# Load queue, PSUM eviction by pairs and a third result buffer in a 7x7 depthwise stage

## The chip, the cores and the metric

The kernel runs on one core of a Trainium2 chip. The metric is the device time of one execution in microseconds. TensorE (PE) multiplies, VectorE (DVE) and ScalarE (ACT) read its results out of PSUM, GpSimd (POOL) moves data inside SBUF, and SyncE (SP) issues DMAs. SP, ACT and POOL each have a DMA queue of their own; all three queues are served by the same 16 DMA engines.

## The reference

Two layers on one image of 384 channels of 192x192 in float32. The first is a group norm, a 1x1 convolution, a 2x2 max pool, a 3x3 depthwise convolution and a channel attention. The second, which the change touches, is a group norm and a 7x7 depthwise convolution with symmetrised weights:

```python
    x = x + _L0_conv_ref(_gn(x), ...)
    # --- layer 1 (conv_preact) ---
    x = x + _L1_conv_ref(_gn(x), L1_conv_weight)

    def _L1_conv_ref(x, weight):
        w_sym = (weight + jnp.rot90(weight, k=1, axes=(2, 3)) + jnp.rot90(weight, k=2, axes=(2, 3)) + jnp.rot90(weight, k=3, axes=(2, 3))) * 0.25
        return _dwconv(x, w_sym, STRIDE, PAD)
```

## The kernel before, in words

The first layer takes about 2490 us and ends by writing the sum x to DRAM twice: `sd` holds it in the order that the 7x7 stage wants (128 rows of "column phase and image row", each with 384 channels of 300 numbers), and `sh` holds the halo rows. The 7x7 weights lie in DRAM as `wt`, one banded matrix of 128x384 per channel.

The 7x7 stage runs 48 steps of eight channels. For each channel, three float32 matmuls (L825, L830, L836; each of them is two passes of the PE array) add up one result of 128x288 in PSUM: two multiply the weights with shifted views of the main operand, the third multiplies with `aux`, which holds halo rows and a constant row. Two channels share one PSUM tile `pc` of two banks, and there are four such tiles, one for each pair q of a step.

Step n does this, in the order in which the code records it (`keep` holds each engine to this order):

- The loads for step n+2 are issued: `w` (L677, 1536 KB, 128 pieces of 12,288 bytes), `main` (L682, 1200 KB, 128 pieces of 9,600 bytes) and two halo loads into `aux` (L687, 281 KB each, 30 pieces of 9,600 bytes). There are three buffers of each.
- POOL prepares step n+1 (`borders`, L749 to L770): it adds the mean at the borders of `main` and `aux` and copies a part of `main` into `aux`.
- POOL turns the results of step n-1 into rows (`spread`, two copies from `apart` to `res`, L794), and eight stores write them out (L798, 144 KB each in pieces of 768 bytes; `res` has two buffers).
- PE computes the four pairs. Each pair is read out of PSUM in four parts of 32 partitions (g = 0 to 3) that are scaled and stored in `apart`; DVE takes g = 0 and 2 (L849), ACT takes g = 1 and 3 (L847). `apart` has two buffers.
- After the second pair, DVE adds the identity to the weights of step n+1 (`middle`, L784).

All loads and stores of this stage are on SP's queue, so SP issues w, main, two halos, eight stores, w, main and so on. A DMA reports its end on one of eight semaphores that are handed round in turn; a DMA that gets a semaphore still in use waits, before it is issued, for the DMA eight places earlier to land. In the program before, a step has twelve DMAs, and the fifth to eighth store of a step wait in this way for the landing of that step's w, main and halos.

Of the kernel before, what the change touches and what calls it, by code (L numbers as in the profile page):

```python
# [8 lines left out]
F32 = mybir.dt.float32  # L9
# [4 lines left out]
P = 128  # L14
# [38 lines left out]
NT = HW // TR  # L53
CP = 4
NJ = HW // CP
# [19 lines left out]
def conv_preact_d2(  # L75
# [17 lines left out]
    nc = tc.nc  # L93
# [10 lines left out]
    sd = dram.tile([CP * TR, C, RUN], F32, name="sd")  # L104
# [3 lines left out]
    wt = dram.tile([P, C, 3 * P], F32, name="wt")  # L108
# [13 lines left out]
    for kt in range(KT):  # L122
        g = gsel[:, kt, :].rearrange("p (g j) -> p g j", j=GC)
# [136 lines left out]
    with ExitStack() as bx:  # L260
# [70 lines left out]
        for r in range(3):  # L331
            row = []
            for ct in range(CT):
                t = padp.tile([P, PR + 2, PS + 2], F32, name=f"pad{r}_{ct}")
# [208 lines left out]
    with ExitStack() as dx:  # L543
# [8 lines left out]
        for i in range(4):  # L552
            t = sxp.tile([P, LEAD + CP * RB * RUN + LEAD], F32, name=f"sx{i}")
# [97 lines left out]
    with ExitStack() as ex_:  # L651
# [3 lines left out]
        outp = ex_.enter_context(tc.tile_pool(name="outp", bufs=2))  # L655
        auxs = []
        for i in range(3):
            t = wide.tile([P, CB, NT, JP], F32, name=f"aux{i}")
# [10 lines left out]
        keep = tc.keep_in_program_order  # L669
        steps = C // CB  # L670

        def span(n):
            return slice(n * CB, (n + 1) * CB)

        def load_w(n):
            w = wtp.tile([P, CB, 3 * P], F32, name=f"w{n}", tag="w")
            keep(nc.sync.dma_start(w, wt[:, span(n)]))  # L677
            return w

        def load_main(n):  # L680
            main = mainp.tile([P, CB, NT, JP], F32, name=f"main{n}", tag="main")
            keep(nc.sync.dma_start(main.rearrange("p c t j -> p c (t j)"), sd[:, span(n)]))  # L682
            aux = auxs[n % len(auxs)]
            af = aux.rearrange("p c t j -> p c (t j)")
            for base, h in ((TOP, 0), (BOT, HALO)):
                keep(
                    nc.sync.dma_start(  # L687
                        af[base : base + HALO * NQ], sh[h * NQ : (h + HALO) * NQ, span(n)]
                    )
                )  # L690
            return main, aux

        ws = {n: load_w(n) for n in range(2)}
        mains = {n: load_main(n) for n in range(2)}

        mean1, rstd1, _ = group_stats(st.rearrange("p t b n s -> p t (b n) s"), "1")
# [17 lines left out]
        with tc.tile_pool(name="mps", bufs=1, space=PSUM) as mps:  # L714
            rows = []
            for name, v in (("mb", mean1), ("sb", std1), ("rb", rstd1)):
                t = wide.tile([P, C], F32, name=name)
# [23 lines left out]
        def borders(n):  # L741

            main, aux = mains[n]
            cs = span(n)

            def border(t, lo, hi, j, k, nj):
                part = t[lo:hi, :, :, j : j + nj]
                keep(
                    nc.gpsimd.tensor_tensor(  # L749
                        part, part,  # L750
                        mm[lo:hi, cs, k : k + nj].unsqueeze(2).to_broadcast(
                            [hi - lo, CB, NT, nj]
                        ),
                        ALU.add,
                    )
                )

            border(main, 0, P, 0, 0, 1)
            border(main, 0, P, NJ, 1, 2)
            keep(  # L760
                nc.gpsimd.tensor_copy(
                    aux[0:TOP, :, :, 0:NJ].rearrange("p c t j -> p (c t) j"),
                    main[0:TOP, :, :, 2 : 2 + NJ].rearrange("p c t j -> p (c t) j"),
                )
            )
            border(aux, TOP, ONE, 0, 3, 1)
            border(aux, TOP, ONE, NJ - 1, 4, 1)
            for base, t in ((TOP, 0), (BOT, NT - 1)):
                keep(
                    nc.gpsimd.tensor_copy(  # L770
                        aux[base : base + HALO * NQ, :, t, 0:NJ],
                        mb[base : base + HALO * NQ, cs].unsqueeze(2).to_broadcast(
                            [HALO * NQ, CB, NJ]
                        ),
                    )
                )

        def middle(n):

            for i in range(0, CB, 4):  # L780
                c = n * CB + i
                mid = ws[n][:, i : i + 4, CENTRE : CENTRE + P]
                keep(
                    nc.vector.scalar_tensor_tensor(  # L784
                        mid, eye.unsqueeze(1).to_broadcast([P, 4, P]), stdb[:, c : c + 1], mid,
                        ALU.mult, ALU.add,
                    )
                )

        def spread(n, apart):  # L790

            res = outp.tile([P, 2, NT * NJ, CP], F32, name=f"res{n}", tag="res")
            for k in range(2):
                keep(nc.gpsimd.tensor_copy(res[:, k], apart[:, :, k].rearrange("p e n -> p n e")))  # L794
            for k in range(2):
                for q in range(CP):
                    keep(
                        nc.sync.dma_start(  # L798
                            out[n * CB + 2 * q + k].rearrange("(t r) w -> r t w", t=NT),
                            res[q * TR : (q + 1) * TR, k].rearrange(  # L800
                                "p (t j) e -> p t (j e)", t=NT
                            ),
                        )
                    )
# [4 lines left out]
        for n in range(steps):  # L809
            if n + 2 < steps:  # L810
                ws[n + 2] = load_w(n + 2)
                mains[n + 2] = load_main(n + 2)
            if n + 1 < steps:
                borders(n + 1)
            if last is not None:
                spread(n - 1, last)
            w, (main, aux) = ws.pop(n), mains.pop(n)
            apart = outp.tile([P, CP, 2, NT * NJ], F32, name=f"apart{n}", tag="apart")
            for q in range(CP):
                ps = pc.tile([P, 2, 512], F32, name=f"pc{n}_{q}", tag="pc")  # L820
                for k in range(2):
                    i = 2 * q + k
                    acc = ps[:, k, 0 : NT * NJ]
                    keep(
                        nc.tensor.matmul(  # L825
                            acc, w[:, i, 0:P], main[:, i, :, 0:NJ], start=True, stop=False
                        )
                    )
                    keep(
                        nc.tensor.matmul(  # L830
                            acc, w[:, i, P : 2 * P], main[:, i, :, 1 : 1 + NJ],
                            start=False, stop=False,
                        )
                    )
                    keep(
                        nc.tensor.matmul(  # L836
                            acc, w[0:KLAST, i, 2 * P :], aux[0:KLAST, i, :, 0:NJ],
                            start=False, stop=True,
                        )
                    )  # L840
                c = n * CB + 2 * q
                for g in range(CP):
                    src = ps[g * TR : (g + 1) * TR, :, 0 : NT * NJ]
                    dst = apart[q * TR : (q + 1) * TR, CP - 1 - g]
                    scale = rb[g * TR : (g + 1) * TR, c : c + 1]
                    if g % 2:
                        keep(nc.scalar.mul(dst, src, scale))  # L847
                    else:
                        keep(nc.vector.tensor_scalar_mul(dst, src, scale))  # L849
                if q == 1 and n + 1 < steps:  # L850
                    middle(n + 1)
            last = apart
# [57 lines left out]
```

## Time and profile before

| what | value |
|---|---|
| median of 3 runs | 3200.5 us (3199.22 to 3203.96) |
| the profiled execution | 3205.75 us, of which its span is 3204.1 us |
| 7x7 stage, first matmul to end of span | 2534.1 to 3204.1 us |
| PE over the span | 84% busy |
| DVE, ACT, POOL over the span | 77%, 23%, 25% busy |
| DMA on SP's queue | 395.82 MB, 35.7% of the 16 engines' span |

Busy time is time in which an engine executes; waits and DMA issues are not in it. The DMA share is the mean busy share of the 16 DMA engines. The profiled execution is 5.25 us above the median of the runs, so a difference worked out in its trace is applied to the median.

### The profile page before, as it was taken

What the parts mean: (1) busy time and instruction counts of PE and PEld (TensorE: products, weight loads), DVE (VectorE), ACT (ScalarE), POOL (GpSimd) and SP (SyncE); (2) the same over time, 40 slices, a digit from 0 to 9 for tenths busy, and PEclk for the clock granted to TensorE, in tenths of its full rate; (3) what the DMA queues carried; (4) which work ended last, traced back from release to release, by engine and by line L of the source; (5) the groups of instructions that cost most, each with busy time, mean ns of one, the idle gap of its engine ahead of it and who ended that gap; (6) DMA issues with size and microseconds to landing.
All of it is one profiled execution on the core that took longest, in us unless ns stands there. A gap on an engine that the chain in (4) does not pass through costs nothing. (4 is left out here: it accounts for less than half of the span.)

```text
span 3204.1 us, 25358 instructions
## 1 busy us (share of the span) xinstructions
PE 2698.8 (84%) x8243; PEld 1529.8 (48%) x8243; DVE 2466.5 (77%) x3993; ACT 740.1 (23%) x1545; POOL 804.1 (25%) x959
## 2 busy tenths in 40 slices
PE   0079999999999999999999998355784599898997
PEld 0044444444444444444444444234562476666665
DVE  7957878888888877778888888775999676656665
ACT  0001222222222222222222222011211144434443
POOL 0044343100000000000000001143122366667666
PEclk9999999999999999999999999577997699999998
DMA  9946666311111111111111000399999699999998
GB/s 376 372 138 229 208 215 223 103 40 61 46 37 37 37 37 37 37 38 39 38 37 53 27 8 14 124 392 391 362 364 314 213 325 333 320 317 332 328 322 272
DMA packets 205379, 576.50 MB, mean 180 GB/s; under 512 B 18672, under 2 KB 131680, under 8 KB 190080
## 3 DMA queue, kind: packets, MB, share of 16 engines
q1 hardware_dynamic: 156496, 395.82, 35.7%
q0 software_dynamic: 43776, 175.52, 15.8%
q10 hardware_dynamic: 4976, 3.56, 0.3%
q8 instruction: 66, 1.08, 0.1%
q14 instruction: 65, 0.53, 0.1%
HBM read 341.56 MB, written 233.10 MB: 179 GB/s over the span
## 5 line engine op out<-in xcount | busy, mean ns | idle before, releaser
L348 PE MATMUL pq<-xq,wq 128*128 128x512 f32 x3402 | 1474.0, 592 | 0.0
L348 PEld LDWEIGHTS pq<-xq,wq 128*128 128x128 f32 x3402 | 640.0, 190 | 773.5 <-issue 719.2
L384 DVE SCALAR_TENSOR_TENSOR qk<-pad,wd,qk 128x384 f32<-128x384 f32 x1152 | 690.6, 617 | 52.9 <-ACT pad L363 40.7
L355 DVE TENSOR_REDUCE t<-pq 128x128 f32<-128x512 f32 x648 | 444.9, 687 | 253.4 <-PE pq L348 253.4
L849 DVE TENSOR_SCALAR apart<-pc,rb 32x576 f32<-32x576 f32 x384 | 311.1, 810 | 245.3 <-ACT apart L847 156.7
L438 POOL DMA_DIRECT2D vd<-vb x72 | 57.7, 802 | 1350.4 <-DVE vb L384 1350.4
L847 ACT ACTIVATE apart<-pc,rb 32x576 f32<-32x576 f32 x384 | 281.7, 734 | 446.1 <-DVE apart L849 362.3
L384 DVE SCALAR_TENSOR_TENSOR vb<-pad,wd,vb 128x384 f32<-128x384 f32 x576 | 337.5, 614 | 20.5 <-ACT pad L363 18.5
L836 PE MATMUL pc<-aux,w 127*128 127x288 f32 x768 | 262.1, 423 | 42.4 <-POOL aux L770 42.3
L363 ACT ACTIVATE pad<-t,bq 128x96 f32<-128x96 f32 x207 | 77.9, 376 | 931.6 <-DVE t L355 931.6
L608 DVE TENSOR_TENSOR sx<-xr,y 128x576 f32<-128x576 f32 x192 | 222.3, 1212 | 74.9 <-ACT y L597 39.1
L825 PE MATMUL pc<-main,w 128*128 128x288 f32 x768 | 260.3, 421 | 19.5 <-DVE w L784 9.6
L830 PE MATMUL pc<-main,w 128*128 128x288 f32 x768 | 258.6, 419 | 0.0
L348 PE MATMUL pq<-xs,wq 128*128 128x512 f32 x486 | 215.3, 603 | 0.0
L794 POOL COPY res<-apart 128x1152 f32<-128x1152 f32 x96 | 210.0, 2220 | 18.6 <-ACT apart L847 8.2
L577 PE MATMUL po<-v,attnT 128*128 128x288 f32 x448 | 126.6, 438 | 89.3 <-DMA v<-vd 84.0
L836 PEld LDWEIGHTS pc<-aux,w 127*128 127x128 f32 x768 | 150.1, 198 | 96.2 <-POOL aux L770 54.1
L190 PE MATMUL gs<-mv,gsel 128*128 128x1 f32 x36 | 8.5, 353 | 220.9 <-DVE mv L180 218.0
L825 PEld LDWEIGHTS pc<-main,w 128*128 128x128 f32 x768 | 149.2, 196 | 70.4 <-POOL res L794 11.7
L590 PE MATMUL pr<-gl,wp 128*128 128x288 f32 x576 | 154.4, 424 | 32.1 <-ACT y L597 32.0
L830 PEld LDWEIGHTS pc<-main,w 128*128 128x128 f32 x768 | 149.9, 195 | 45.1
L615 DVE BATCH_NORM_STATS2 st<-sx 128x6 f32<-128x288 f32 x384 | 149.8, 474 | 0.2
(128 smaller groups left out, 2044.9 us busy)
## 6 DMA issues: line engine op xcount, KB each, us to landing
w<-wt SPq DMA_DIRECT2D x48, 1536.0 KB, 6.8
sd<-sx POOLq DMA_DIRECT2D x96, 600.0 KB, 10.2
main<-sd SPq DMA_DIRECT2D x48, 1200.0 KB, 11.7
xs<-in_x_dram SPq DMA_DIRECT2D x24, 2304.0 KB, 11.6
xr<-in_x_dram SPq DMA_DIRECT2D x48, 1152.0 KB, 27.1
out_dram<-res SPq DMA_DIRECT2D x384, 144.0 KB, 7.2
xq<-in_x_dram SPq DMA_DIRECT2D x21, 2304.0 KB, 8.2
wt<-g POOLq DMA_DIRECT2D x24, 1152.0 KB, 6.7
```

The source lines that it names most:

```text
L348: nc.tensor.matmul(ps, wq[:, kt, ct * P : (ct + 1) * P], rows[:, kt, :, g * 64 : (g + 1) * 64], start=(kt == 0), stop=(kt == KT - 1),)
L355: nc.vector.tensor_reduce(t[:, :, g * 32 : (g + 1) * 32], ps.rearrange("p (h a w b) -> p h w a b", h=PR, a=2, b=2), AX.XY, ALU.max,)
L384: nc.vector.scalar_tensor_tensor(dst, win, w, dst, ALU.mult, ALU.add)
L590: nc.tensor.matmul(ps[:, h, 0:H], wp[:, ct, ot * P : (ot + 1) * P], gl[:, ct, h * H : (h + 1) * H], start=(ct == 0), stop=(ct == KT - 1),)
L608: nc.vector.tensor_tensor(sx[:, v, :, :, dj : dj + NJ], xq[:, :, :, :, e], y[:, :, :, e // 2].unsqueeze(1).to_broadcast([P, RB, NT, NJ]), ...
L615: nc.vector.bn_stats(st[:, ot, b, v * RB + a, :], sx[:, v, a, :, dj : dj + NJ])
L794: keep(nc.gpsimd.tensor_copy(res[:, k], apart[:, :, k].rearrange("p e n -> p n e")))
L825: nc.tensor.matmul(acc, w[:, i, 0:P], main[:, i, :, 0:NJ], start=True, stop=False)
L830: nc.tensor.matmul(acc, w[:, i, P : 2 * P], main[:, i, :, 1 : 1 + NJ], start=False, stop=False,)
L836: nc.tensor.matmul(acc, w[0:KLAST, i, 2 * P :], aux[0:KLAST, i, :, 0:NJ], start=False, stop=True,)
L847: keep(nc.scalar.mul(dst, src, scale))
L849: keep(nc.vector.tensor_scalar_mul(dst, src, scale))
```

## The change

Three edits in the 7x7 stage. The loads of `w` and `main` are issued by ACT instead of SP; halo loads and stores stay with SP. `apart` gets a third buffer. The four parts of a pair are all read out by one engine: DVE for pairs 0 and 2, ACT for pairs 1 and 3.

```diff
         def load_w(n):
             w = wtp.tile([P, CB, 3 * P], F32, name=f"w{n}", tag="w")
-            keep(nc.sync.dma_start(w, wt[:, span(n)]))
+            keep(nc.scalar.dma_start(w, wt[:, span(n)]))
             return w
 
         def load_main(n):
             main = mainp.tile([P, CB, NT, JP], F32, name=f"main{n}", tag="main")
-            keep(nc.sync.dma_start(main.rearrange("p c t j -> p c (t j)"), sd[:, span(n)]))
+            keep(nc.scalar.dma_start(main.rearrange("p c t j -> p c (t j)"), sd[:, span(n)]))
...
-            apart = outp.tile([P, CP, 2, NT * NJ], F32, name=f"apart{n}", tag="apart")
+            apart = outp.tile([P, CP, 2, NT * NJ], F32, name=f"apart{n}", tag="apart", bufs=3)
...
-                    if g % 2:
+                    if q % 2:
                         keep(nc.scalar.mul(dst, src, scale))
                     else:
                         keep(nc.vector.tensor_scalar_mul(dst, src, scale))
```

In the built program the instructions of PE and POOL stand in the same order as before. ACT's order in a step becomes: issue w(n+2), issue main(n+2), four parts of pair 1, four parts of pair 3. SP's becomes: two halos (n+2), eight stores (n-1). The eight semaphores are handed round in the order halo, w, halo, store 1, main, stores 2 to 8, so that w(n+2) is issued only after the second store of the group before has landed, main(n+2) after its fifth, and the fifth store of a group after that group's first halo, the sixth after its w.

## The prediction

> **What bounds the kernel now.** I read the strip of 40 slices first: from slice 32 on the DMA row stands at 9 and PE at 8 to 9. So I asked for the 7x7 stage alone: busy time by stretch, its DMA queues and issues, and the waits of SP, PE, DVE and ACT.
>
> ```profile
> core 0: us, PE busy (x) PEld busy (x) DVE busy (x) ACT busy (x) POOL busy (x), PEclk, DMA share, GB/s
> 2600.00:2800.00 200.00, 182.02 (x713) 136.28 (x711) 134.23 (x150) 87.82 (x120) 130.17 (x129) 0.97 1.00 326
> 2800.00:3000.00 200.00, 179.07 (x678) 133.76 (x679) 118.06 (x142) 82.48 (x113) 133.65 (x132) 0.94 1.00 325
> 3000.00:3160.00 160.00, 144.82 (x553) 108.54 (x553) 95.09 (x115) 67.57 (x93) 104.72 (x101) 0.95 1.01 329
> ...
> q1 hardware_dynamic: 81745, 182.52, 100.0%
> ...
> w<-wt SPq DMA_DIRECT2D x40, 1536.0 KB, 6.8
> main<-sd SPq DMA_DIRECT2D x40, 1200.0 KB, 11.7
> out_dram<-res SPq DMA_DIRECT2D x320, 144.0 KB, 7.4
> aux<-sh SPq DMA_DIRECT2D x80, 281.2 KB, 12.0
> ```
>
> The reader is to see: all 16 DMA engines are busy all the time (1.00), with SP's queue alone, at 325 to 329 GB/s. A step moves 4.57 MB, so it lasts 14.0 us (w to w in SP's timeline: 2617.30 to 3163.14 in 39 steps). The other engines have room: PE's shortest step is 11.8 us (the last one, 3179.2 to 3191.0), DVE, ACT and POOL are busy 62%, 42% and 66% of these 560 us.
>
> The waits show what DVE and ACT lose to each other, and what holds PE and SP:
>
> ```profile
> ACT apart L847 <- DVE apart L849: 314.7, 247, 4.8
> ...
> DVE apart L849 <- ACT apart L847: 132.2, 162, 0.9
> DVE apart L849 <- POOL res L794: 71.1, 32, 4.6
> ...
> PE pc L836 <- POOL aux L770: 41.9, 23, 3.1
> ```
>
> ```profile
> SPq L798 <- DMA main<-sd: 151.5, 42, 5.8
> SPq L798 <- POOL res L794: 142.6, 50, 5.5
> SPq L798 <- DMA aux<-sh: 49.4, 76, 1.7
> ```
>
> No row has PE waiting for an eviction (L847 or L849). PE waits for POOL's work on halos that landed late. SP's stores wait for loads to land.
>
> How well are the DMA engines used? I counted the trace's DMA packets from 2600 to 3160 us. Pieces of 12,288 bytes (w) take 460 ns at the median and 545 ns in the mean, pieces of 9,600 bytes (main and halos) 366 and 485 ns (361 at the fastest), and 768 bytes (stores) 36 and 40 ns. By the shortest times a step would be (128 x 0.460 + 188 x 0.361 + 1536 x 0.036)/16 = 11.4 us, and 0.1 us for semaphore writes. The 2.5 us above that are 0.7 in w, 1.5 in the 9,600-byte pieces (main's run at 361 to 370 ns, the halos at 600 to 970 ns where they run) and 0.3 in stores. Fewer than 16 packets are in flight in 13% of the time; taken over the engines that is 2.0% of them idle, 0.28 us per step.
>
> **The change part by part.**
>
> *Loads on ACT.* SP loses a w and a main issue per step (0.39 and 0.44 us, its rows at 2784.75 and 2785.18) and ACT gains them: with 8 evictions of 0.734 us, ACT has 6.7 us of work in a step of 14.0. Bytes and pieces stay. Two queues now hold work at once. The trace has such a place, the stretch before, where SP loads xr and POOL stores sd:
>
> ```profile
> 2260.00:2300.00 40.00, 36.92 (x151) 28.05 (x150) 40.00 (x67) 8.05 (x12) 8.98 (x12) 1.00 1.04 354
> ...
> q1 hardware_dynamic: 4376, 7.25, 54.5%
> q0 software_dynamic: 1610, 6.87, 49.5%
> ```
>
> While both queues are full there, packets go one for one whatever their size (in the us from 2289: 59 of 4,800 bytes, 58 of 1,536). So beside w and main, which have 16 pieces per engine, only about 16 of a step's 96 store pieces per engine get through; the rest goes after. That delays stores but leaves no engine idle.
>
> What waits on ACT: w(n+2) for the second store of the previous group, main(n+2) for its fifth. Behind them stand ACT's evictions of step n, and for those wait PE (the pc tiles of pairs 1 and 3) and POOL's res copies. A store alone takes 2.1 us from issue to landing (3196.55 to 3198.63). When the second store lands, up to six more of 0.44 us each (12 pieces of 36 ns) are queued or about to be, 2.6 us of work; a load needs 1.0 us from that landing to its first packet (0.1 wake-up, 0.4 issue, some 0.5 to the first packet, as after the issue at 3196.55). So the DMA engines have cover, and PE has 14.0 - 11.8 = 2.2 us of slack per step. I therefore cost these waits at nothing; without that cover they cost the 1.0 us per step.
>
> The gain is in idle engines. Before, the next w came only after the eighth store was issued, which waited for the second halo (2798.97 landed, 2799.46 w issued), and the engines that were done early had nothing. Now w needs the second store only, and main follows it with no gap. Bounds: 0 to the whole 0.7 us by which w's pieces exceed 460 ns. I take 0.28 us, the idle time counted above, as the row nearest to it: 45 steps x 0.28 = -12.6 us. That two queues slow the pieces is bounded by the two-queue stretch: from 2210 to 2330 us its 4,800-byte pieces took 210 ns (192 at the median), its 1,536-byte ones 74 (65), 9% and 14% above the median, against 10% and 18% for stores and w in one queue now. So I take 0; the bound is 7% of the 7.4 us in which loads and stores mix, +0.5 us per step. The halos still follow the stores on SP's queue and still run mostly among themselves: 0, bounds -0.7 (half of their excess hidden) and +0.5.
>
> A rule speaks against any gain. The Trainium skill, "DMA: Bandwidth & Descriptors", section "Issuing engines are not separate DMA queues", says that DMAs issued from several engines end on the same 16 DMA engines and interleave, so that only the sequencer's issue time is saved. The share of 1.00 with one queue fits it, the 1.04 with two does not quite. By the rule alone the gain would be nothing and the sum +3 us.
>
> *Start of the stage.* w(3) was issued by SP at 2548.47, as the first step's matmuls ended. On ACT it stands behind the four parts of pair 3, 4 x 0.77 = +3.1 us, once; the DMA queue is nearly empty there, so I count +3. Bounds 0 and +3.1.
>
> *Eviction by pairs.* The hand-overs vanish (314.7 us of ACT's idle time, 132.2 of DVE's). Gain on the path: 0, because PE waits for no eviction and the DMA engines set the step. A pair now takes 4 x 0.81 = 3.2 us on DVE or 3.1 on ACT, each engine has two pairs in a step, and with `middle` DVE has 8 us of 14. Without DMA as cover it would be worth at most 2.2 us per step, since PE's 11.8 comes next. In the tail, from the last matmul (3191.0) to the last eviction (3194.3), four parts take 3.1 us instead of 3.3: 0.
>
> *Third apart buffer.* It removes DVE's wait for the res copy (71.1 us). Nobody waited for DVE: 0.
>
> Sum: -12.6 + 3 = -9.6 us. The profiled execution would go from 3205.75 to 3196.2; it stands 5.25 us above the median, so the forecast is 3200.5 - 9.6 = 3191 us.
>
> **The rivals.**
>
> *More comes back.* If w loses its whole excess (0.7) and half of the halos' excess is hidden beside other pieces (0.7), a step is 1.4 us shorter: 45 x 1.4 - 3 = -60 us, 3141 us. For it: 2.2 us of slack on PE. Against: the halo pieces are slow where they run together, two groups of 30 partitions each, and the order on SP keeps them together. Half of it gives 3170.
>
> *Slower: loads wait for stores that starve.* ACT issues a load only after certain stores have landed, and stores get one small piece per large one. If the backlog on SP's queue is used up when the load's condition is met, 1.0 us per step lies open and the 0.28 isn't won: +45 + 3 = +48, 3249 us. It decides once the backlog behind the store waited for is under 1.0 us, some two stores. For it: the res copies hold stores back already (SP waits 142.6 us for L794). Against: six stores and the halos normally follow.
>
> *No change.* The step is bytes over a saturated set of engines: +3 us, 3203.
>
> **How the numbers follow.** A difference of 0.2% (6.4 us) is about what a measurement here can tell. Chances: the forecast 0.45 (own range 3171 to 3209, by 0.7 us gained or 0.2 lost per step), more gain 0.17, slower 0.28, no change 0.10. Of the forecast's case 0.26 lies below 3194, 0.11 within 0.2%, 0.08 above; no change gives 0.07 same and 0.03 slower. So faster 0.43, same 0.18, slower 0.39. The range 3150 to 3248 leaves out the end of the large gain and the worst of the slow case.
>
> **What would show it.** Right: DMA share still 1.00, steps of 13.7 to 13.8 us and 329 to 335 GB/s between 2600 and 3150, no hand-over waits between DVE and ACT, PE still waiting only for POOL or loads, w issued by ACT with a wait for a store before it. Wrong: a DMA share below 0.97 with ACT waiting long for stores (the slower rival), PE waiting for L847 (evictions held up behind a load's issue), halo pieces with another mean time (contention changed), or steps near 12 us with PE as the bound.

## The result: 1.1% slower

| kernel | median | runs | profiled execution |
|---|---|---|---|
| before | 3202.2 us | 3199.2 to 3204.4, 4 runs | 3205.75 us, span 3204.1 |
| changed | 3237.2 us | 3230.1 to 3245.6, 4 runs | 3240.19 us, span 3238.5 |

The ratio is 1.0111 with a 95% interval of 1.0083 to 1.0139. The forecast was 3191 us, 0.3% faster; the change costs 35 us. All of it is in the 7x7 stage, which grew from 670.0 to 704.6 us in the profiled executions (first matmul at 2534.1 and 2533.9 us). From the start of step 8 to that of step 46 a step takes 14.71 us instead of 13.92, and 46 steps of 0.79 us are 36 us. PE itself is no slower: its shortest step takes 11.83 us in both.

**The profile after.** The first view is the stage by stretches (columns: busy time and count of PE, PEld, DVE, ACT and POOL, then granted clock, DMA share, GB/s). It answers to the view that opened the prediction:

```profile
2600.00:2800.00 200.00, 170.74 (x650) 128.59 (x650) 115.79 (x137) 79.22 (x108) 115.59 (x121) 0.93 0.90 311
2800.00:3000.00 200.00, 174.33 (x664) 130.88 (x663) 117.76 (x139) 81.20 (x111) 120.52 (x126) 0.94 0.92 314
3000.00:3160.00 160.00, 137.33 (x505) 102.44 (x504) 87.55 (x105) 62.56 (x86) 90.04 (x96) 0.91 0.91 306
```

The DMA share fell from 1.00 to 0.91, and every compute engine is less busy too. Nothing is full any more; something waits. Some of the waits of the engines in the same 560 us (waiter, releaser, total us, times, longest):

```profile
POOL aux L749 <- DMA aux<-sh: 225.1, 38, 10.1
DVE apart L849 <- POOL res L794: 92.1, 14, 10.1
PEld pc L836 <- POOL aux L770: 91.2, 30, 5.6
PE pc L836 <- POOL aux L770: 73.8, 25, 5.2
DVE apart L849 <- ACT apart L847: 21.6, 8, 2.7
```

The hand-overs between DVE and ACT, 447 us before, are down to 21.6. PE still waits for POOL's border work, 73.8 us instead of 41.9, and POOL now waits for the halos (L749 on `aux`, 225.1 us), where it waited for `main` before (L749 on `main`, 161.5 us; no such row after). So the halos come late. SP's queue says why:

```profile
SPq L798 <- DMA w<-wt: 261.9, 37, 10.7
SPq L687 <- DMA main<-sd: 60.9, 35, 3.4
```

A store (L798) writes `res` and has no use for `w`; a halo load (L687) has no use for `main`. Yet SP spends 58% of these 560 us waiting for loads of ACT's queue. The data ask for no such wait; what is left is the completion semaphore, on which a DMA reports its end. The trace gives the semaphore of each issue, and the DMAs of SP and ACT take theirs from the same eight numbers (100 and 102 to 108); this is one turn of the changed kernel (start in us, queue, DMA, number of its semaphore):

```
2786.33  ACT  w             104
2786.75  ACT  main          107
2787.60  SP   fifth store   103
2793.74  SP   sixth store   104   same as w
2794.10  SP   seventh store 105
2794.58  SP   eighth store  106
2796.93  SP   first halo    107   same as main
2797.31  SP   second halo   100
```

The sixth store gets the semaphore of the w that ACT issued one microsecond before the fifth, and waits until that w has landed. The first halo of the next group gets main's. Between 2600 and 3150 us this holds for 36 of 37 steps (sixth store and w) and for 35 of 36 (first halo and main). Such a wait, which comes from the semaphore and not from the data, is called a tie below.

**A correction.** The last sentences of the section on the change put this turn in the wrong place. They take the w and main in a group to be those of the step that its halos belong to. In the changed program w and main run ahead: the group holds the halos of step k, the stores of step k-3, and w and main of step k+2, just issued. So the sixth store waits for a load that is new, not for one that has long been under way, and the halos of step k+1 stand behind it. Measured from issue to the step's first matmul, mean of steps 8 to 45, w leads by 29.2 us (15.4 before) and the first halo by only 3.8 (14.5 before).

The chain that ended last walks through this (start us, us, what):

```profile
2786.33 0.33 ACTq L677
...
2786.75 10.11 DMA main<-sd
...
2796.93 0.34 SPq L687
2797.26 0.04 issue
2797.31 0.40 SPq L687
...
2799.16 3.86 DMA out_dram<-res
...
2803.05 0.52 POOL aux L770
2803.57 0.04 issue
2803.61 0.51 PE pc L836
```

One link of this view is put down wrongly. It goes from the halos over three stores and the landing of the third (2799.16) to POOL's L770. The waits for stores that stand just before that L770 carry line L794: they belong to the copies into `res` that come after it. POOL's timeline has the border work begin when the halos land:

```profile
2801.88 0.56 POOL L749 TENSOR_TENSOR aux<-aux,mm 62x48 f32<-62x48 f32 x2 [4.29 <-DMA aux<-sh]
```

PE ends step k-1; that frees the w buffer, and ACT issues w and main of step k+2 (2786.33, 2786.75). Main lands after 10.11 us. Only then does SP issue the halos of step k+1 (2796.93); they land, POOL finishes the borders (2803.05), and PE goes on with step k+1 (2803.61), whose last matmul ends at 2814.6. At 2814.68 ACT issues the w of step k+4. This loop covers two steps: 10.5 us from w's issue to main's landing, 6.8 from there to PE, 11.0 for PE's step, 28.3 in all, 14.2 per step here and 14.71 in the mean. Two such loops, for odd and even steps, run interleaved. PE's 11.0 us are work; the rest is one wait for a landing after another, while the DMA engines, at a share of 0.91, are not full.

### The profile page after: what moved, and what is told of

Read it like the earlier page. It is cut to its first block, busy times and chain, and to the rows that moved or that the text cites. A ratio compares the mean times of both kernels' runs of the same rounds, so it can differ in the third digit from the quotient of the medians.

```text
span 3238.5 us, 25457 instructions
## 1 busy us (share of the span) xinstructions
PE 2702.0 (83%) x8243; PEld 1531.8 (47%) x8243; DVE 2461.4 (76%) x3993; ACT 741.2 (23%) x1545; POOL 782.0 (24%) x959
## 5 line engine op out<-in xcount | busy, mean ns | idle before, releaser
L384 DVE SCALAR_TENSOR_TENSOR vb<-pad,wd,vb 128x384 f32<-128x384 f32 x576 | 337.7, 614 | 20.5 <-ACT pad L363 18.5
L825 PE MATMUL pc<-main,w 128*128 128x288 f32 x768 | 263.0, 425 | 4.2 <-POOL aux L749 4.2
L794 POOL COPY res<-apart 128x1152 f32<-128x1152 f32 x96 | 208.4, 2201 | 18.3 <-ACT apart L847 15.5
L825 PEld LDWEIGHTS pc<-main,w 128*128 128x128 f32 x768 | 153.3, 200 | 51.1 <-POOL aux L749 4.4
## 6 DMA issues: line engine op xcount, KB each, us to landing
xr<-in_x_dram SPq DMA_DIRECT2D x48, 1152.0 KB, 28.3
```

Of the source, the lines that this page charges most:

```text
L384: nc.vector.scalar_tensor_tensor(dst, win, w, dst, ALU.mult, ALU.add)
L825: nc.tensor.matmul(acc, w[:, i, 0:P], main[:, i, :, 0:NJ], start=True, stop=False)
```

## The experiments

Two theories stood against each other. **Semaphores**: the eight completion semaphores that SP's and ACT's DMAs share in turn tie SP's stores and halos to ACT's loads, and the loss is this chain. **Two queues**: loads on one queue and stores on another serve each other worse in the DMA engines, whatever the semaphores. A third candidate, the eviction or the buffer, is separated first. "Lead" is the time from an issue to the first matmul of its step, and leads and the length of a step are means over steps 8 to 45 (from 0); ratios are to the kernel before, run on the same chip beside each kernel. The windows of the views, and of the mean times of pieces, are 2600 to 3150 us.

### The queues alone, the eviction alone

The first has only this part of the change, the second all but this part:

```diff
-            keep(nc.sync.dma_start(w, wt[:, span(n)]))
+            keep(nc.scalar.dma_start(w, wt[:, span(n)]))
...
-            keep(nc.sync.dma_start(main.rearrange("p c t j -> p c (t j)"), sd[:, span(n)]))
+            keep(nc.scalar.dma_start(main.rearrange("p c t j -> p c (t j)"), sd[:, span(n)]))
```

> Only the queue change: w and main issued by ScalarE, eviction shared by parts as before, two apart buffers. Theory A (halos come late because they stand on SP behind a store that waits, through a shared completion semaphore, for a w that ScalarE has only just issued): the loss comes with the queues, so 3215 to 3240 us, DMA share below 0.97 between 2600 and 3150 us, and POOL waiting over 100 us for aux<-sh. Here the semaphores fall so that the sixth store of a group waits for a w one step ahead of its halos, not two, so the loss may be smaller than the full 35 us. Theory B (the loss comes from evictions that stand behind loads on ScalarE, or from pair-wise eviction): with parts shared as before within 6 us of 3202 us if pair-wise eviction is the cause.

> Only pair-wise eviction and the third apart buffer, all loads and stores on SP. Theory A: no wait for DMA is touched, so 3202 us within 6 us, DMA share 1.00, hand-over waits between VectorE and ScalarE gone. Theory B (pair-wise eviction delays PE or the res copies): 3215 to 3240 us with PE waiting for L847 or L849.

The queues alone: 3270.5 us beside 3208.5, ratio 1.0184 [1.0167, 1.0201], a step of 15.31 us, more than the 3215 to 3240 us that I expected. The eviction and the third buffer alone: 3209.3, ratio 0.9999 [0.9986, 1.0012]. The loss comes with the queues. The eviction and the buffer are worth nothing by themselves. Beside the queue change the whole is 0.7% better than the queues alone, but that is not shown to be their doing: the turn of the semaphores falls differently in the two programs. With the queues alone it is the seventh store that has w's semaphore in 23 of some 36 steps and other DMAs in the rest; in the whole change it is the sixth nearly always. SP's waits in the run with the queues alone:

```profile
SPq L798 <- DMA w<-wt: 250.6, 34, 11.2
SPq L687 <- DMA main<-sd: 34.2, 23, 2.4
```

The first halo's lead is 6.1 us there with a standard deviation of 4.7 (3.8 and 1.9 with the whole change). Pieces are not slower than before: w's take 536 ns in the mean (546 before), and in the whole change 514.

### The halos on ScalarE as well

```diff
                 keep(
-                    nc.sync.dma_start(
+                    nc.scalar.dma_start(
                         af[base : base + HALO * NQ], sh[h * NQ : (h + HALO) * NQ, span(n)]
```

> The changed kernel with the halo loads on ScalarE's queue too, so that SP has the stores alone. Theory A: halos are issued with their w and main, two steps before use, and no longer stand behind a waiting store; the chain from w over main, halo and POOL to PE is gone, the DMA share returns to 0.98 to 1.00 and the time to 3202 us or below (3150 to 3205). Theory C (two queues make the transfers themselves slower, by packets that alternate between loads and stores or by slower halo pieces): 3225 us or more, with a DMA share of 1.00 and longer packets.

3431.7 us, ratio 1.0691 [1.0675, 1.0707], a step of 18.5 us and a DMA share of 0.73. My expectation for the semaphores missed by far: I had thought that with all loads on one queue the ties would fall out. They change sides. Now a halo on ACT has the semaphore of a store of SP, and ACT's evictions stand behind it:

```profile
ACT apart L847 <- DMA out_dram<-res: 258.4, 29, 9.5
DVE apart L849 <- ACT apart L847: 220.0, 26, 9.4
POOL res L794 <- issue: 138.7, 30, 5.7
PE pc L825 <- DVE apart L849: 125.7, 59, 3.5
```

This is what the prediction's slower rival had in mind (a load on ACT waits for a store, evictions wait behind it). Where it happens it costs 7%, not the 1.5% of that rival, as late evictions hold up DVE's part of the work and PE (L825), and the res copies (L794) come late too, and with them the very stores that are waited for. (The view puts the wait before L794 down to "issue"; in the trace the copy at 2796.56 us begins 0.1 us after ACT's last eviction of its step, and SP waits 339.1 us of 550 for such copies.)

### The halos a step earlier

The changed kernel with a fourth `aux` buffer, the halos of step n+3 issued ahead of the loads of n+2:

```diff
-        for i in range(3):
+        for i in range(4):
...
+            if n + 3 < steps:
+                load_halos(n + 3)
```

> The changed kernel with four aux buffers and each halo load issued one step earlier on SP, still behind the waiting store. Theory A: the halos keep their late place in the queue but have a step of 14 us in hand, so POOL's wait for aux<-sh falls from 236 us to under 60 us and the time to 3160 to 3205 us. Theory C (transfers slower): the time stays at 3225 us or more.

3315.1 us, ratio 1.0328 [1.0312, 1.0343]: missed as well. The halos were helped as I had thought: POOL's wait for them, 225.1 us in the changed kernel, is gone from its rows. But the tie to w stays, and SP's stand-still moves everything behind it:

```profile
SPq L805 <- DMA w<-wt: 287.0, 32, 13.2
SPq L687 <- DMA main<-sd: 52.2, 31, 4.0
```

The lead of the halos rises by only 3.7 us, to 7.5; the stores of step k, first to eighth, slip to 44 to 57 us after the issue of w of step k+3 (26 to 37 in the changed kernel). So the buffers of `res` come free late, POOL's copies wait for them, and PE waits for the border work behind the copies:

```profile
POOL res L801 <- DMA out_dram<-res: 124.3, 20, 9.9
PE pc L845 <- POOL aux L777: 66.4, 29, 3.0
```

These two misses left the theory unproven: I could say after the fact where each tie had gone, but not remove it. The next runs remove it.

### Eight DMAs in a step instead of twelve

Two channels are stored by one DMA: the same bytes in the same pieces of 768 bytes, four stores instead of eight. With eight DMAs per step for eight semaphores, each DMA follows its own forerunner of the step before, and but for four DMAs in the window none on SP is tied to a load. The same edit on the kernel before is the control.

```diff
-            for k in range(2):
-                for q in range(CP):
+            for q in range(CP):
...
-                            out[n * CB + 2 * q + k].rearrange("(t r) w -> r t w", t=NT),
-                            res[q * TR : (q + 1) * TR, k].rearrange(
-                                "p (t j) e -> p t (j e)", t=NT
+                            out[n * CB + 2 * q : n * CB + 2 * q + 2].rearrange(
+                                "k (t r) w -> r (k t) w", t=NT
+                            ),
+                            res[q * TR : (q + 1) * TR].rearrange(
+                                "p k (t j) e -> p (k t) (j e)", t=NT
```

> The changed kernel with the result stored by four DMAs per step instead of eight (two channels in one DMA; the same bytes, the same pieces of 768 bytes, the same queues). A step then has eight DMAs for the eight shared completion semaphores, so each DMA takes the semaphore of its own forerunner of the step before: no store and no halo has to wait for a w or a main any more, and no load for a store. Theory (the loss is in these shared semaphores): SP's wait for w (276.6 us in 590) and for main (62.7) vanish, halo0 is issued 12 us or more ahead of its step (3.8 in the changed kernel), the DMA share is 0.97 or more, a step 13.0 to 13.95 us, and the time 3160 to 3210 us. Rival (two queues that hold loads and stores at once serve each other worse, whatever the semaphores): the time stays at 3230 to 3275 us and the DMA share near 0.91, with SP or ACT waiting for something else.

> The kernel before with the same four stores per step, all loads on SP. It shows what four larger stores are worth by themselves. Theory: on one queue the shared semaphores follow the queue's own order, so little hangs on them: DMA share 1.00, step 13.8 to 14.0 us, 3195 to 3220 us (a store now needs both res copies, 3 us later than one; four issues of 0.44 us less per step on SP). Rival (the eight stores were themselves a cost, and what the run of four stores in the changed kernel gains is due to that): 20 us or more under the time of the kernel before, here as there.

The changed kernel with four stores: 3223.9 beside 3218.5, ratio 1.0006 [0.998, 1.0032], where the changed kernel had 1.0111. The loss is gone, but the gain that I expected (3160 to 3210) isn't there; the runs spread from 3197.7 to 3235.6, and the profiled one took 3215.2. The kernel before with four stores: 3247.8, ratio 1.0091 [1.0064, 1.0118]. So four stores alone do harm on one queue (I had expected none: SP waits 237.7 us for the res copies, since a store now needs both, and the next loads stand behind), and the change, without the ties, makes good 0.85 of these 0.91%. Stretches of the changed kernel with four stores, then SP's longest waits:

```profile
2600.00:2800.00 200.00, 180.55 (x714) 138.62 (x713) 125.00 (x149) 87.78 (x120) 134.17 (x136) 0.95 1.01 335
2800.00:3000.00 200.00, 182.39 (x720) 139.63 (x720) 124.97 (x151) 87.82 (x120) 131.02 (x131) 0.95 1.01 338
```

```profile
SPq L797 <- DMA out_dram<-res: 136.7, 80, 8.2
SPq L797 <- POOL main L749: 91.1, 35, 5.9
SPq L687 <- PE pc L837: 40.0, 17, 5.2
```

No wait for w is left and 4.8 us for main; the share is 1.01 and the halo's lead 15.8 us.

### The ties put back by four tiny stores

On top of the changed kernel with four stores, four stores of 64 bytes per step to a scratch area. They move 256 bytes beside 4.56 MB (a piece took a DMA engine 10 ns in the mean), but bring the step back to twelve DMAs, the third of them tied to w and the fourth to main.

```diff
+                keep(
+                    nc.sync.dma_start(
+                        pad[4 * n + q : 4 * n + q + 1, 0:16], mb[0:1, 16 * q : 16 * q + 16]
+                    )
+                )
```

> The run of the changed kernel with four stores per step (3224 beside 3218 for the kernel before), plus four stores of 64 bytes per step on SP, one after each store, to a scratch area in DRAM. They add no bytes to speak of, but bring the DMAs of a step back to twelve, so that the turn of the eight completion semaphores is what it is in the changed kernel: the third tiny store waits for the w just issued, the fourth for its main, and the next step's halos stand behind both on SP. Theory (the shared semaphores are the cause): SP waits for w and main again by 150 us or more in 550, halo0 leads its step by less than 7 us instead of 15.8, a step is 14.1 to 14.9 us instead of 13.57, and the time 3245 to 3285 us. Rival (four larger stores are what helped, or the semaphores are harmless): four issues of 0.44 us on SP, which has room, 3220 to 3235 us.

3277.1 us beside 3212.0, ratio 1.0202 [1.017, 1.0234]; without the tiny stores it was 1.0006. A stretch, and SP's waits (L808 are the tiny stores, L688 the halos):

```profile
2800.00:3000.00 200.00, 166.49 (x623) 124.44 (x622) 109.29 (x130) 75.58 (x104) 111.56 (x117) 0.91 0.89 296
```

```profile
SPq L808 <- DMA w<-wt: 267.4, 37, 10.2
SPq L808 <- DMA main<-sd: 93.9, 34, 4.0
```

The waits are back to the size that they have in the changed kernel, the halo's lead is 3.4 us, a step 15.38 us instead of 13.57 (I had expected 14.1 to 14.9), the share 0.89. The third tiny store has w's semaphore in 35 steps of the window and the fourth main's in 34. The four issues take SP 1 to 2 us per step; its waits for w take 7.2 us each in the mean. Four DMAs that carry next to nothing cost 2%, because of whose semaphore they take. This is the strongest evidence for the semaphores.

### The loads on GpSimd instead of ScalarE

GpSimd's DMAs have semaphores of their own (111 to 118 in the trace). The split of loads and stores is that of the change; only the queue of w and main is another:

```diff
-            keep(nc.scalar.dma_start(w, wt[:, span(n)]))
+            keep(nc.gpsimd.dma_start(w, wt[:, span(n)]))
...
-            keep(nc.scalar.dma_start(main.rearrange("p c t j -> p c (t j)"), sd[:, span(n)]))
+            keep(nc.gpsimd.dma_start(main.rearrange("p c t j -> p c (t j)"), sd[:, span(n)]))
```

> The changed kernel with w and main issued by GpSimd instead of ScalarE; halos and stores stay on SyncE. The loads are on a queue of their own as in the changed kernel, but GpSimd's DMAs have semaphores of their own, and SP's ten DMAs share the eight among themselves only: no store or halo waits for a load. Theory: SP no longer waits for w or main, the halos follow the stores freely, a step is 13.4 to 14.1 us and the time 3180 to 3225 us beside 3212 for the kernel before (the uncertain part: GpSimd waits for PE before it issues w, with its border work behind). Rival (loads on one queue and stores with halos on another delay each other in the DMA engines, whatever the semaphores): 3235 to 3275 us as with ScalarE.

3175.1 us beside 3203.9, ratio 0.9908 [0.9887, 0.9929], at the good end of what was expected. The same split that loses 1.1% on ScalarE wins 0.9% on GpSimd. SP's longest waits and two stretches:

```profile
SPq L687 <- DMA out_dram<-res: 91.2, 48, 3.3
SPq L798 <- DMA out_dram<-res: 40.9, 26, 6.3
SPq L798 <- DMA aux<-sh: 23.7, 36, 2.3
```

```profile
2600.00:2800.00 200.00, 186.26 (x739) 141.78 (x739) 138.28 (x156) 89.02 (x123) 151.26 (x166) 0.97 1.02 344
2800.00:3000.00 200.00, 178.98 (x704) 135.93 (x703) 133.74 (x146) 86.54 (x119) 149.90 (x163) 0.95 0.99 339
```

No SP wait for a w or a main is among its rows, the share is back at 1.0, a step takes 13.38 us. With this and the tiny stores the theory of two queues falls: here the DMA engines serve loads and stores from two queues at 339 to 344 GB/s, against 325 before.

### The halos on GpSimd

```diff
                 keep(
-                    nc.sync.dma_start(
+                    nc.gpsimd.dma_start(
                         af[base : base + HALO * NQ], sh[h * NQ : (h + HALO) * NQ, span(n)]
```

This edit was made on the changed kernel, on that with a third `res` buffer, on the kernel before, and on the kernel before with the change's eviction and third `apart` buffer.

> The changed kernel with the two halos of a step issued by GpSimd, whose DMAs have semaphores of their own; w and main stay on ScalarE, the stores on SyncE. The halos then hang on no load, while some stores still wait for a w just issued (ten DMAs for eight semaphores). Theory: the chain main landed, then halo issued is cut, halo0 leads its step by more than 8 us, a step is 13.7 to 14.2 us, and the time is 3190 to 3225 us, with GpSimd's own time for two issues per step (it is busy for 0.58 of the stage) as the uncertain part. Rival (three queues compete): 3240 us or more.

> The run with the halos on GpSimd (3190 beside 3218) with a third res buffer. There POOL waited 99.9 us of 550 for res buffers whose stores had not landed. Theory: the DMA share is 1.00, so the transfers set the step and POOL's wait is cover that nobody needs; the time stays within 10 us, 3180 to 3200 us beside 3218 for the kernel before. Rival (POOL's wait delays the border work for the next step, for which PE waited 64 us): a step loses 0.5 us or more, 3165 to 3178 us.

> The kernel before with only the halos moved, to GpSimd; w, main and stores stay on SP, the eviction and the buffers as before. It tells what the gain of the run with halos on GpSimd (3190 beside 3218) is due to. If it is due to w and main on a queue of their own, running two steps ahead without the ties that hold back the halos, this run gives none of it: 3208 to 3225 us, w issued 15 us ahead of its step. If it is due to the halos alone (their pieces beside others, on a queue with semaphores of its own), it gives all of it: 3185 to 3198 us, halo pieces at 560 ns instead of some 620.

> The kernel before with the halos on GpSimd (3170 beside 3212) and, in addition, this change's eviction by pairs and third apart buffer; w, main and stores stay on SP. There a step is 12.83 us, near PE's floor of 11.83, and PE waits for POOL and DVE only. Theory A (the transfers still set the step, share 1.00 in two of three stretches): the eviction is worth nothing here either, within 8 us of 3170 beside 3212. Theory B (with transfers quicker, DVE's hand-overs now reach PE through w's L784, 34.2 us in 550, and L825 behind it, 41.0): 0.3 us per step or more is won, 3145 to 3160 us.

| kernel, with halos on GpSimd | median | before beside it | ratio, 95% | step |
|---|---|---|---|---|
| changed kernel | 3190.4 | 3218.5 | 0.9923 [0.9898, 0.9948] | 13.03 us |
| changed kernel, third res | 3196.1 | 3212.0 | 0.9958 [0.9941, 0.9976] | 13.38 us |
| kernel before | 3169.6 | 3212.0 | 0.9876 [0.9847, 0.9905] | 12.83 us |
| before + eviction, third apart | 3159.7 | 3203.9 | 0.9866 [0.9838, 0.9893] | 12.77 us |

All four beat the kernel before, by 0.4 to 1.3%. In the first, SP's stores still wait for w, and it is the w and main on ScalarE that cost: the last kernel is the first with these two loads back on SP, and it is 0.6% faster (0.9866 against 0.9923; the two were run on different chips, each beside its own kernel before). SP's waits in the first:

```profile
SPq L798 <- DMA out_dram<-res: 188.9, 89, 9.3
SPq L798 <- DMA w<-wt: 138.8, 39, 6.6
```

The third res buffer brings nothing, as expected. The eviction brings nothing even at 12.83 us per step, within the bounds set for it. The kernel before with its halos moved was faster than either of my cases for it. Two stretches of it:

```profile
2600.00:2800.00 200.00, 185.84 (x749) 141.54 (x747) 146.08 (x156) 91.59 (x125) 151.77 (x171) 0.99 1.00 349
2800.00:3000.00 200.00, 189.29 (x760) 143.91 (x761) 145.21 (x160) 93.78 (x128) 156.31 (x178) 0.99 1.02 370
```

The DMA share is what it was before the change, 1.00, but 349 to 370 GB/s pass instead of 325. (The third stretch, 3000 to 3150, already holds the end of the loads: 0.95 and 329.) Each piece is quicker: w's take 497 ns in the mean (546 before), the halos 558 (by an estimate 730 before: 188 pieces of 9,600 bytes at 485 in the mean, less main's 128 at some 369). That is (128 x 49 + 60 x 172)/16 = 1.04 us per step, and the step lost 1.09. The halos are issued 3.9 us before their w here, 0.9 us after it before. Whether it is this place among the others, or the ten DMAs per step on SP in place of twelve, that shortens the pieces, these runs don't separate.

## Why the prediction was wrong, by its own steps

*What bounds the kernel.* Right for the kernel before: its DMA engines were full, PE waited for POOL and not for an eviction. But it took a share of 1.00 as something that the change could only improve on. (A step moves 4.56 MB, not 4.57; nothing hangs on it.)

*Loads on ACT: the waits.* This step failed. It looked at what the loads would wait for ("w(n+2) for the second store of the previous group, main(n+2) for its fifth") and costed that at nothing. So far this was right: ACT has no wait for a store among the rows of the changed kernel. It did not follow the same turn of semaphores in the other direction, to the stores and halos on SP that take the semaphores of w and main. The list was even written down in the section on the change, with the fifth and sixth store waiting for a halo and a w, but with the wrong step for that w, which made the wait look long over. Measured: SP waited 261.9 + 60.9 us of 560 for w and main, and a step took 0.79 us more where the sum had 0 for these waits.

*"The halos still follow the stores on SP's queue and still run mostly among themselves: 0."* The order is as said, but the time of it is not: the first halo went from 0.9 us after its step's w to 25.3 us after it. The bounds of -0.7 to +0.5 us were taken from the speed of the pieces alone and could not hold a late issue. That is the general fault of the sum: it counted what each transfer takes and not when it may start.

*The gain of 0.28 us per step from idle engines, and two queues slowing the pieces by 0.* Nothing speaks against the second: w's pieces take 514 ns in the changed kernel (546 before), 768 bytes 39 (40). The first didn't come, since the engines were idle for 9% of the time and not for 2%. Without the ties a gain does come, and a larger one: 0.54 us per step with the loads on GpSimd.

*Start of the stage: +3.* Too much: the w of step 3 came 14.8 us after the first matmul instead of 14.4, and the first four steps lost 0.5 us together.

*Eviction by pairs, third buffer: 0.* Right: 0.9999 [0.9986, 1.0012] alone. What makes the whole change 0.7% better than the queues alone, these edits or the other turn of semaphores that comes with them, stays open.

*The rule of the Trainium skill.* "DMA: Bandwidth & Descriptors", section "Issuing engines are not separate DMA queues", makes a gain from another queue only the issue time. By it alone my estimate was +3 us. It was nearer than my sum (-9.6 us; measured +35), but what happened isn't in it: in these runs the choice of the issuing engine moved the kernel from 6.9% slower to 1.2% faster with the same bytes. What each DMA had to wait for before it was issued differed, and so did how long the pieces took.

*The slower rival* named a DMA share below 0.97, and that came; its mechanism, loads on ACT that wait for starved stores, did not. Its 3249 us is near the measured 3237 by chance. Its mechanism exists in the run with the halos on ScalarE as well, which is 7% slower.

## What to carry to other kernels

Before moving a DMA to another queue, write down for both queues which semaphore each DMA takes and whose landing it then waits for, with the step each belongs to: a DMA whose issue waits for something that its data do not need is the sign. In these runs a queue whose DMAs draw on other semaphores, or a number of DMAs per step that lets each one follow its own forerunner, removed the tie; an early load on one queue is no gain if it holds up a late one on another. A DMA share of 1.00 was no floor either (325 and 349 to 370 GB/s at the same share): look at how long a piece takes beside the shortest of its kind.

## What was unexpected of the hardware

- A DMA share of 1.00 went with 325 GB/s and with 349 to 370 GB/s for the same pieces. Busy engines were not engines at their best.
- Taken together, pieces got no slower when loads and stores came from two queues at the same time. With w and main on GpSimd the 768-byte pieces took 37 ns in the mean (40 on one queue), main's 371 and the halos' 572 (485 for both together on one queue), but w's took 573 (546). Summed over the pieces of a step and divided by 16 engines that is 13.3 us, where the kernel before has 13.9.
- In the kernel before with its halos on GpSimd, a halo issue took 0.51 us of POOL's time (41.4 us for 82), a little more than on SP (0.34 to 0.44). With these 1.0 us per step POOL's share rose to 0.76, and yet PE's wait for the border copies (L770) fell from 40.2 to 1.5 us of 550. The longest wait in PE's rows there is for DVE's `middle` (L784), 34.2 us; that of the weight loads is for POOL's res copies (L794), 41.0 us, so POOL isn't out of PE's way altogether.
